# Splitting the last superblock of a graph-attention kernel into two single quads

## The chip, the cores and the metric

The kernel runs on one core of a Trainium2 chip. The metric is the device time of one execution in microseconds; a kernel's figure is the median of several runs. The core has five engines with a queue of instructions each: PE (TensorE, matrix products), DVE (VectorE), ACT (ScalarE), POOL (GpSimd) and SP (SyncE, which here issues transfers). An engine works through its queue in order and waits on semaphores for what other engines and transfers have finished.

## The reference

One layer of graph attention with a residual: 12,500 nodes of 128 values, 200,000 edges sorted by destination, four heads of 32 values.

```python
h = relu(layernorm(x))
hn = (h @ W_node.T).reshape(N, 4, 32);  e = (edge_attr @ W_edge.T).reshape(E, 4, 32)
att = sum(concat([hn[src], hn[dst], e], -1) * a, -1)      # one value per edge and head
att = where(att > 0, att, 0.2 * att)
m = maximum(segment_max(att, dst), 0.0)
ex = exp(att - m[dst])
denom = segment_sum(ex, dst) + (E - deg)[:, None] * exp(-m)   # deg: edges per destination
out = x + segment_sum((ex / denom[dst])[:, :, None] * hn[src], dst).reshape(N, 128)
```

## The kernel before

**Tiling.** The edges are cut into 392 groups of 511 (and one slot that carries the unfinished sum of the group before). Four groups are a quad (QG), so there are 98 quads, 0 to 97. A group's destinations lie in a window of 96 nodes. Quads are joined into superblocks, listed in `supers`: two of two quads, twenty of four, then 3, 3, 2, 2, 2, 2. A superblock is the unit of one softmax.

**Stages.** A first part writes a table of node rows to DRAM (h W_node and the attention terms). Then each quad goes through these steps:

- `fetch` (L472): SP loads edge attributes, destinations and the windows of x; POOL issues 16 indirect gathers, four per group, of the source nodes' rows into one of eight buffers `ga` (L137). The gathers of quad q+2 are asked for in `open_logits(q)`, and a buffer is filled again when the group that used it eight quads before is through.
- `all_logits` (L724): per group DVE compares the destinations (L500) and PE adds the destination and edge terms into `lg` (L505, L508). `flush` then calls `add_sources` (L511), which reduces `lg` (L520) and adds the gathered source term (L522) into `U`. L522 therefore waits until the quad's gathers have landed. `flush` runs at the start of the next `all_logits`, or, where there is none, at the start of the softmax.
- `softmax` (L533), once per superblock: a comparison of neighbouring destinations (`kp`, L542), transposes on PE (L547), the slope on ACT (L549), scans on DVE (L556, L566, L578, L581, L584), exponentials on ACT (L590, L593) and transposes back (L601 to L613). It yields four times between, so that other steps stand in the engines' queues among its parts.
- `sums` (L668): per group DVE scales the gathered rows (L687) and makes the one-hot marks of destinations (L691); PE sums three quarters of the group (L696). `complete_group` (L630) then adds the carry of the group before (DVE L635, ACT L639), does the last quarter (L640) and copies the result out (ACT L641). For the last two quads (FREE) POOL makes the marks (L664) early, and the carry is read from PSUM.
- `divide` (L701): denominators and quotients on DVE (L708 to L716), the addition of x (L720, on POOL for quads 95 and 96, on DVE otherwise), and one output transfer per group on SP (L722). The windows overlap, so an output is issued only when the one before it has landed. A quad's division comes in the step after its last group; the last quad is divided group by group. Each division takes a tile `res` of its own, of which there are two.

**Order.** The queues' order is written out by hand in the loop over `supers` (L795 to L811), with `together` taking one part of each step in turn. Beside the softmax of a superblock stand the sums of the quad before it and the logits of the first quad of the next superblock; beside the other sums stand the logits of the next superblock's other quads. At the end, before the change: sums of 94 beside logits of 97; sums of 95 beside the softmax of 96 and 97; sums of 96; sums of 97; outputs.

Of the kernel before, what the change touches and what calls it, by code (L numbers as in the profile page):

```python
# [8 lines left out]
F32 = mybir.dt.float32  # L9
# [9 lines left out]
D = H * HD  # L19
# [10 lines left out]
WIN = 96  # L30
QG = 4
# [15 lines left out]
def kernel(  # L47
# [51 lines left out]
    part = consts.tile([P, 1], F32, name="part")  # L99
# [20 lines left out]
    nq = len(quads)  # L120
# [27 lines left out]
    with tc.manual_schedule():  # L148
# [10 lines left out]
        with tc.tile_pool(name="prep", bufs=1) as prep, tc.tile_pool(  # L159
            name="prep_ps", bufs=1, space=bass.MemoryType.PSUM  # L160
# [127 lines left out]
        with tc.tile_pool(name="node", bufs=2) as node, tc.tile_pool(  # L288
            name="node_ps", bufs=2, space=bass.MemoryType.PSUM
        ) as node_ps, tc.tile_pool(name="index", bufs=1) as index, tc.tile_pool(  # L290
            name="index_ps", bufs=1, space=bass.MemoryType.PSUM
# [45 lines left out]
            ends = [3, 6]  # L337
# [88 lines left out]
    per = SBG // QG  # L426


    ends = [2, 2], [3, 3, 2, 2, 2, 2]
    amid = max(nq - sum(ends[0]) - sum(ends[1]), 0)  # L430
    supers = []
    for m in ends[0] + [n for _, n in blocks(amid, per)] + ends[1]:
# [5 lines left out]
    with tc.tile_pool(name="work", bufs=2) as work, \  # L438
            tc.tile_pool(name="turned", bufs=1) as turned, \
            tc.tile_pool(name="ps", bufs=1, space=bass.MemoryType.PSUM) as ps:  # L440
        XW, LG, AT, U, DR = {}, {}, {}, {}, {}
# [10 lines left out]
        def groups(s):  # L452
            q0, m = supers[s]
            g0 = quads[q0][0]
            return g0, quads[q0 + m - 1][0] + quads[q0 + m - 1][1] - g0

        def window(g):
            return nc.values_load(
                base[0:1, g:g + 1], engines=[mybir.EngineType.SP], min_val=0, max_val=N - 1,
                skip_runtime_bounds_check_because="a destination, which is a node")  # L460
# [11 lines left out]
        def fetch(q):  # L472
            if q not in EA:
                fetch_edges(q)
            fetch_windows(q)
            if q not in GA:
                gather(q, table, ROW)
# [33 lines left out]
        def add_sources(q):  # L511

            s = of_quad[q]
            g0, m = quads[q]
            s0, sm = groups(s)
            if s not in U:
                U[s] = turned.tile([P, J, SBG * H], F32, name="U", bufs=2)
            u = U[s][:, :, 0:sm * H].rearrange("p j (h g) -> p g j h", h=H)[:, g0 - s0:g0 - s0 + m]
            st = work.tile([P, QG, J, H], F32, name="st")
            nc.vector.tensor_reduce(st[:, :m], LG[q][:, :m].rearrange("p g j k h -> p g j h k"),  # L520
                                    AX.X, OP.add)
            nc.vector.tensor_tensor(u, st[:, :m], GA[q][:, :m, :, R_SRC:R_SRC + H], op=OP.add)  # L522
            for kept in (EA, DB, PW, AT, LG):
                del kept[q]
# [8 lines left out]
        def softmax(s):  # L533


            g0, m = groups(s)
            u = U.pop(s)
            R = m * H
            dr = DR.pop(s)

# [1 line left out]
            nc.vector.tensor_tensor(kp[:R, 1:GE], dr[:R, 1:NE + 1], dr[:R, 0:NE], op=OP.is_equal)  # L542
            nc.vector.memset(kp[:R, GE:GE + 1], 0.0)
            same, same_next = kp[:R, 1:GE], kp[:R, 2:GE + 1]
            t_ps = ps.tile([SBG * H, GE], F32, name="t_ps")
            for j in range(J):
                nc.tensor.transpose(t_ps[:R, j * P:(j + 1) * P], u[:, j, :R], ident)  # L547
# [15 lines left out]
            ends = turned.tile([1, H, SBG + 1], F32, name="ends")  # L563
# [66 lines left out]
        def complete_group(q, i, ga, hot, pt, acc, fc):  # L630
            g0, m = quads[q]
            g = g0 + i
            if g:
                before = state["before"]
                nc.vector.tensor_tensor(  # L635
                    ga[0:1, i, 0, 0:H * HW].rearrange("p (h w) -> p h w", w=HW),
                    before[WIN:WIN + 1, 0:H * HW].rearrange("p (h w) -> p h w", w=HW),
                    fc.unsqueeze(2).to_broadcast([1, H, HW]), op=OP.mult)
                nc.scalar.copy(ga[0:1, i, 0, R_CNT:R_CNT + 1], before[WIN:WIN + 1, R_CNT:R_CNT + 1])  # L639
            nc.tensor.matmul(acc, hot[:, i, 0, :], ga[:, i, 0, :], start=False, stop=True)  # L640
            nc.scalar.copy(pt[:, i, :], acc)  # L641
            state["before"] = acc if q >= nq - FREE else pt[:, i, :]

            if i == m - 1 or q == nq - 1:
                lo = i if q == nq - 1 else 0
                den = work.tile([WIN, QG, H], F32, name="den")
                nc.scalar.activation(den[:, lo:i + 1, :], pt[0:WIN, lo:i + 1, R_SRC:R_SRC + H],
                                     AF.Exp, scale=-1.0)
                state["division"] = q, pt, den, lo, i + 1
# [1 line left out]


        FREE = 2
        HOT = {}

        def marks(q):

            g0, m = quads[q]
            hot = work.tile([P, QG, J, WIN + 1], F32, name="hot", bufs=3)
            nc.scalar.copy(hot[:, :m, :, WIN], is_last[:, g0:g0 + m, :])  # L660
            if q >= nq - FREE:
                for i in range(m):
                    for j in range(J):
                        nc.gpsimd.tensor_scalar(hot[:, i, j, 0:WIN], lane, slot[:, g0 + i, j:j + 1],  # L664
                                                None, op0=OP.is_equal)
            return hot

        def sums(q):  # L668
# [8 lines left out]
            pt = work.tile([WIN + 1, QG, ROW], F32, name="pt", bufs=3)  # L677
            hot = HOT.pop(q) if q in HOT else marks(q)
            for i in range(m):
                nc.scalar.copy(ga[:, i, :, R_SRC:R_SRC + H], heads(xs)[:, :, :, g0 - s0 + i])  # L680
            for i in range(m):
                g = g0 + i
                if q == nq - 1 - FREE and i == 1:
                    for k in range(FREE):
                        HOT[nq - FREE + k] = marks(nq - FREE + k)
                val = ga[:, i, :, 0:H * HW].rearrange("p j (h w) -> p j h w", w=HW)
# [14 lines left out]
        def divide(q, pt, den, lo, hi):  # L701

            n = hi - lo
            xw = XW[q][:, lo:hi]
            pt = pt[0:WIN, lo:hi]
            den = den[:, lo:hi]
            others = work.tile([WIN, QG], F32, name="others")
            nc.vector.tensor_scalar(others[:, :n], pt[:, :, R_CNT], -1.0, float(E),  # L708
                                    op0=OP.mult, op1=OP.add)
            nc.vector.tensor_tensor(den, den, others[:, :n].unsqueeze(2).to_broadcast([WIN, n, H]),  # L710
                                    op=OP.mult)
            val = pt[:, :, 0:H * HW].rearrange("p g (h w) -> p g h w", w=HW)
            nc.vector.tensor_tensor(den, den, val[:, :, :, HD], op=OP.add)
            nc.vector.reciprocal(share_ps[:, :n, :], den)
            res = work.tile([WIN, QG, D], F32, name="res")
            nc.vector.tensor_tensor(  # L716
                res[:, :n, :].rearrange("p g (h d) -> p g h d", d=HD), val[:, :, :, 0:HD],
                share_ps[:, :n, :].unsqueeze(3).to_broadcast([WIN, n, H, HD]), op=OP.mult)
            add = nc.gpsimd if nq - 1 > q >= nq - 1 - FREE else nc.vector
            add.tensor_tensor(res[:, :n, :], res[:, :n, :], xw, op=OP.add)  # L720
            for i in range(n):
                nc.sync.dma_start(out[bass.ds(window(quads[q][0] + lo + i), WIN), :], res[:, i, :])  # L722
# [9 lines left out]
        def flush():  # L732

            if "logits" in state:
                add_sources(state.pop("logits"))
# [43 lines left out]
            nc.vector.tensor_copy(flag, worst[:, 2:3])  # L779
            yield  # L780

        def softmax_next(s):
            flush()
            yield from softmax(s)

        with tc.manual_schedule():
            for q in range(min(2, nq)):
                fetch(q)
            on_vector = nc.vector.tensor_copy
            together(*late(0, on_vector), normed(1))  # L790
            together(*late(1, on_vector), all_logits(0), normed(2))
            for q in range(1, supers[0][1]):
                together(all_logits(q), raw_statistics(raw_pool, 3))
            check_steps = checked()
            for s, (q0, m) in enumerate(supers):  # L795


                ahead = list(range(q0 + m, sum(supers[s + 1]))) if s + 1 < len(supers) else []
                now, ahead = ahead[:1], ahead[1:]
                together(*([sums(q0 - 1)] if s else late(2) + [raw_scaled(3)]),  # L800
                         *map(all_logits, now), softmax_next(s))
                for k in range(m - 1):
                    now, ahead = ahead[:1], ahead[1:]
                    together(sums(q0 + k), *map(all_logits, now))
                    if s > 4:
                        next(check_steps, None)
                for a in ahead:
                    together(all_logits(a))
                if not s:
                    complete()  # L810
                    together(*late(3))  # L811
            flush()
            together(sums(nq - 1))
            complete()
            complete()
            together(check_steps)
            redo = nc.values_load(flag[0:1, 0:1], min_val=0, max_val=1)
# [197 lines left out]
```

## Time and profile before

| what | value |
|---|---|
| median of 3 runs | 2048.64 us (2042.75 to 2051.03) |
| the profiled execution: own time, span | 2566.17 us, 2564.4 us |
| busy: PE, DVE, ACT, POOL | 1396.5, 1360.6, 427.9, 1514.3 us |
| granted PE clock, mean | 0.54 |
| from 300 to 2440 us: DVE busy, POOL busy | 1152.17, 1363.77 us of 2140 |
| from 2443 to 2560 us: DVE busy, POOL busy | 94.27, 19.40 us of 117 |
| last gather issued | 2440.58 us |

The profiled execution is a single one and is longer than the runs that were timed without a profile. Rows and sums from the profile are therefore compared with its own span, and only then with the median. In a row, the figure in brackets is the idle time of the engine before it and what ended it.

### The profile page before, as it was taken

The numbers are of one execution on the slowest core, as the hardware profiler recorded it, in microseconds if no ns is written. First come the engines' busy times: TensorE is split into PE (matmuls) and PEld (weight loads), VectorE is DVE, ScalarE is ACT, GpSimd is POOL, SyncE is SP. The second block draws the span as 40 slices with busy tenths as digits, with TensorE's granted clock in tenths as the row PEclk, the third lists the DMA queues.
The fourth block names the chain that finished last, engine by engine and source line by source line (L and its number), as shares of the span: only waits on it lengthen the run. The fifth ranks groups of instructions, "written<-read, shape, count | busy, mean of one in ns | idle before, by whom it ended". The sixth has DMA issues, their size and how long they took to land.

```text
span 2564.4 us, 29422 instructions
## 1 busy us (share of the span) xinstructions
PE 1396.5 (54%) x7275; PEld 1246.7 (49%) x7275; DVE 1360.6 (53%) x3314; ACT 427.9 (17%) x1777; POOL 1514.3 (59%) x1608
## 2 busy tenths in 40 slices
PE   2441665555555555556555655655555555555485
PEld 1331555554545455445454544554544554544375
DVE  2441565554554555555554654554554564455486
ACT  1441411111111111111111111111111111111122
POOL 7235256666666666666666666666666666666603
PEclk9975655555555555555555555555555555555556
DMA  4342455554554455555455545555544544544430
GB/s 152 98 130 56 113 139 124 128 125 108 131 125 111 106 140 125 129 127 124 117 127 127 124 116 126 124 122 121 122 115 120 126 120 118 123 103 112 102 93 17
DMA packets 214496, 299.12 MB, mean 117 GB/s; under 512 B 86122, under 2 KB 162154, under 8 KB 204915
## 3 DMA queue, kind: packets, MB, share of 16 engines
q1 hardware_dynamic: 162512, 184.97, 27.0%
q0 software_dynamic: 50112, 109.65, 19.7%
q10 hardware_dynamic: 1698, 2.58, 0.3%
q8 instruction: 61, 1.00, 0.2%
q14 instruction: 113, 0.92, 0.1%
HBM read 270.49 MB, written 26.52 MB: 116 GB/s over the span
## 4 chain that ended last, share of the span: by engine, by line
another core or an unknown queue 31%; PE 19%; issue 17%; DVE 15%; ACT 5%; POOL 4%; SPq 2%; DMA 1%; DVEq 0%; ACTq 0%; POOLq 0%
PE acc L696 10%; POOL ga L137 4%; PE lg L508 4%; PE acc L640 3%; DVE at L500 2%; ACT pt L641 2%; DVE res L716 1%; DVE res L720 1%; DVE hot L691 1%; DVE ga L687 1%; DVE run L556 1%; DVE ga L635 1%; PE lg L505 1%; ACT ga L639 1%
## 5 line engine op out<-in xcount | busy, mean ns | idle before, releaser
L137 POOL DMA_INDIRECT ga<-table,srci x1502 | 1433.4, 954 | 925.2 <-issue 404.5
L696 PE MATMUL acc<-ga,hot 128*97 128x137 f32 x2352 | 647.2, 446 | 346.9 <-ACT ga L680 163.7
L696 PEld LDWEIGHTS acc<-ga,hot 128*97 128x97 f32 x2352 | 515.7, 278 | 372.1 <-ACT ga L680 168.5
L635 DVE TENSOR_TENSOR ga<-pt,facs 1x132 f32<-1x132 f32 x384 | 110.7, 288 | 644.1 <-ACT pt L641 466.9
L640 PE MATMUL acc<-ga,hot 128*97 128x137 f32 x784 | 265.6, 442 | 263.1 <-ACT ga L639 127.8
L508 PE MATMUL lg<-wblk,ea 128*128 128x8 f32 x1568 | 407.8, 358 | 0.0
L641 ACT COPY pt<-acc 97x137 f32<-97x137 f32 x392 | 107.1, 273 | 1662.7 <-remote 904.7
L508 PEld LDWEIGHTS lg<-wblk,ea 128*128 128x128 f32 x1568 | 380.4, 308 | 0.0
L505 PEld LDWEIGHTS <-at 96*128 96x128 bf16 x1568 | 215.0, 165 | 295.7 <-DVE at L500 150.5
L640 PEld LDWEIGHTS acc<-ga,hot 128*97 128x97 f32 x784 | 190.7, 279 | 291.8 <-ACT ga L639 142.1
L505 PE MATMUL lg<-pw,at 96*128 96x12 bf16 x1568 | 169.5, 181 | 228.3 <-DVE at L500 123.7
L687 DVE TENSOR_TENSOR ga<-ga,ex_ps 128x528 f32<-128x528 f32 x392 | 270.1, 689 | 42.2 <-remote 35.4
L500 DVE TENSOR_TENSOR at<-const_ps,db 96x512 bf16<-96x512 f32 x392 | 266.9, 682 | 8.9 <-DMA db<-in_dst_dram 3.0
L691 DVE TENSOR_TENSOR hot<-const_ps,slot 128x384 f32<-128x384 f32 x384 | 209.1, 544 | 0.0
L520 DVE TENSOR_REDUCE st<-lg 128x64 f32<-128x192 f32 x98 | 33.7, 344 | 124.7 <-remote 79.9
L375 PE MATMUL row_ps<-wcat,hT 128*128 128x137 f32 x198 | 41.4, 361 | 80.0 <-DVE hT L367 32.8
L601 PE MATMUL ex_ps<-ident,ex 64*128 64x64 f32 (+2 forms) x112 | 18.6, 315 | 110.5 <-ACT ex L590 65.4
L375 PEld LDWEIGHTS row_ps<-wcat,hT 128*128 128x128 f32 x198 | 35.2, 253 | 86.3 <-issue 44.6
L639 ACT COPY ga<-pt 1x1 f32<-1x1 f32 x384 | 72.4, 188 | 10.7
L137 POOL DMA_INDIRECT ga<-in_x_dram,srci x64 | 60.6, 947 | 20.8 <-issue 19.2
L716 DVE TENSOR_TENSOR res<-pt,const_ps 96x512 f32<-96x512 f32 (+1 forms) x101 | 67.3, 667 | 7.1 <-DMA out_dram<-res 3.3
L601 PEld LDWEIGHTS ex_ps<-ident,ex 64*128 64x128 f32 (+2 forms) x112 | 13.8, 208 | 113.5 <-ACT ex L590 67.4
(133 smaller groups left out, 1065.2 us busy)
## 6 DMA issues: line engine op xcount, KB each, us to landing
db<-in_dst_dram SPq DMA_DIRECT2D x98, 768.0 KB
ea<-in_edge_t_dram SPq DMA_DIRECT2D x98, 512.0 KB
ga<-table,srci POOLq DMA_INDIRECT x1502
xw<-in_x_dram SPq DMA_DIRECT2D x392, 48.0 KB
out_dram<-res SPq DMA_DIRECT2D x392, 48.0 KB
pw<-side SPq DMA_DIRECT2D x392, 2.2 KB
table<-row SPq DMA_DIRECT2D x9, 616.5 KB
xt<-in_x_dram SPq DMA_DIRECT2D x9, 576.0 KB
```

What stands on the lines that cost most here:

```text
L137: nc.gpsimd.indirect_dma_start(out=ga[:, i, j, 0:width], out_offset=None, in_=rows, in_offset=bass.IndirectOffsetOnAxis(ap=srci[:, g0 + i, ...
L500: nc.vector.tensor_tensor(at[:, i, :], node_ps[0:WIN, g0 + i:g0 + i + 1].to_broadcast([WIN, GE]), db[:, i, :], op=OP.is_equal)
L505: nc.tensor.matmul(lg[:, i, j].rearrange("p k h -> p (k h)"), at[:, i, j * P:(j + 1) * P], sw, start=i + j == 0, stop=False, skip_group_ch ...
L508: nc.tensor.matmul(lg[:, i, 2 * w:2 * w + 2, 0, :], ea[:, i, w, :], wblk, start=False, stop=True, skip_group_check=True)
L635: nc.vector.tensor_tensor(ga[0:1, i, 0, 0:H * HW].rearrange("p (h w) -> p h w", w=HW), before[WIN:WIN + 1, 0:H * HW].rearrange("p (h w) -> ...
L639: nc.scalar.copy(ga[0:1, i, 0, R_CNT:R_CNT + 1], before[WIN:WIN + 1, R_CNT:R_CNT + 1])
L640: nc.tensor.matmul(acc, hot[:, i, 0, :], ga[:, i, 0, :], start=False, stop=True)
L641: nc.scalar.copy(pt[:, i, :], acc)
L687: nc.vector.tensor_tensor(val, val, heads(ex)[:, :, :, g - s0].unsqueeze(3).to_broadcast([P, J, H, HW]), op=OP.mult)
L691: nc.vector.tensor_tensor(hot[:, i, :, 0:WIN], lane_ps.unsqueeze(1).to_broadcast([P, J, WIN]), slot[:, g, :].unsqueeze(2).to_broadcast([P, ...
L696: nc.tensor.matmul(acc, hot[:, i, j, :], ga[:, i, j, :], start=j == 1, stop=False)
L716: nc.vector.tensor_tensor(res[:, :n, :].rearrange("p g (h d) -> p g h d", d=HD), val[:, :, :, 0:HD], share_ps[:, :n, :].unsqueeze(3).to_br ...
```

## The change

The last superblock of two quads (96 and 97) becomes two of one quad each. The softmax of 96 now stands beside the sums of 95 and the logits of 97, that of 97 beside the sums of 96. In `softmax` the comparison `kp` comes ahead of `flush`, which moves into it. Quad 96 is divided two groups at a time, and the parts of one quad's division write slices of one tile `res` instead of a tile each.

```diff
-    ends = [2, 2], [3, 3, 2, 2, 2, 2]
+    ends = [2, 2], [3, 3, 2, 2, 2, 1, 1]
...
             g0, m = groups(s)
-            u = U.pop(s)
             R = m * H
             dr = DR.pop(s)
...
             same, same_next = kp[:R, 1:GE], kp[:R, 2:GE + 1]
+            flush()
+            u = U.pop(s)
             t_ps = ps.tile([SBG * H, GE], F32, name="t_ps")
...
-            if i == m - 1 or q == nq - 1:
-                lo = i if q == nq - 1 else 0
+            part = 1 if q == nq - 1 else 2 if q == nq - 2 else QG
+            if (i + 1) % part == 0 or i == m - 1:
+                lo = i - i % part
...
-        HOT = {}
+        HOT, RES = {}, {}
...
-            res = work.tile([WIN, QG, D], F32, name="res")
+            if not lo:
+                RES[q] = work.tile([WIN, QG, D], F32, name="res")
+            res = RES[q][:, lo:hi]
...
-        def softmax_next(s):
-            flush()
-            yield from softmax(s)
...
-                         *map(all_logits, now), softmax_next(s))
+                         *map(all_logits, now), softmax(s))
```

## The prediction

> **What bounds the kernel now.** I read the profile's page first, then the waits of the long middle, then the last 120 us row by row. All times below, except the medians, are of the one profiled execution: 2566.2 us, of which the span is 2564.4. The median of the runs is 2048.6, 517 us less. So the first question is which of the rows also hold in a run that nobody records. The fence has two groups of the page (busy, mean ns | idle before, releaser), two lines of the waits from 300 to 2440 us (in total, times, longest), and rows in order of time (start, duration, engine, line).
>
> ```profile
> L137 POOL DMA_INDIRECT ga<-table,srci x1502 | 1433.4, 954 | 925.2 <-issue 404.5
> L641 ACT COPY pt<-acc 97x137 f32<-97x137 f32 x392 | 107.1, 273 | 1662.7 <-remote 904.7
> ...
> ACT pt L641 <- remote: 904.7, 103, 11.8
> POOL ga L137 <- remote: 226.6, 102, 3.3
> ...
> 2391.25 0.40 PE L640 MATMUL acc<-ga,hot 128*97 128x137 f32 x2
> 2399.23 0.27 ACT L641 COPY pt<-acc 97x137 f32<-97x137 f32 x1 [10.14 <-remote]
> ...
> 2386.12 0.94 POOL L137 DMA_INDIRECT ga<-table,srci  x1 [0.30 <-issue]
> 2387.36 0.94 POOL L137 DMA_INDIRECT ga<-table,srci  x1 [0.30 <-issue]
> ...
> 2440.58 0.94 POOL L137 DMA_INDIRECT ga<-table,srci  x1 [0.30 <-issue]
> ```
>
> The reader is to see three things. A gather takes 0.94 us and the next starts 1.25 us after it: 16 gathers, one quad, take 20.0 us of POOL. Once per quad (103 waits for some 94 quads) ACT starts its copy some 9 us late although the matmul it copies (2391.25) ended long before 2399.23, and what it waited for is unknown ("remote"). And those waits stop when the last gather is issued at 2440.58: among the waits after 2443 there is no "remote" row of L641.
>
> Without them the engines need 33 us for two quads: L522 of quad 93 stands at 2450.29, of 95 at 2483.30, of 97 at 2516.41, which is 16.5 us a quad. The median leaves more than that. If the last gather landed 48 us before the end (what the trace shows behind L522 of quad 97), it was at about 2048.6-1.8-48.0 = 1998.8; table gathers start at 160.96 and one wait of 49.0 us for the first free buffer stands at 289.56, so (1998.8-161-49)/1502 = 1.19 us per gather, an estimate, close under the 1.25 of the rows. So I take it that the unrecorded run is paced by POOL's gathers, and that the late copies are the recording's.
>
> Here a rule is weighed. The Trainium skill, NOTIFIC — the notification-queue block, section Overflow, says that a record queue which is full may stall the engine that produces the records. The trace agrees only in that the stalls come with the heavy traffic; no run here shows their cause. With the rule, the end is paced by gathers and my sum is -3 us; without it, engines set the end as in the trace and the sum is +4.
>
> **The end, as recorded.** These are rows in order of time; those without shapes are of the chain that ended last.
>
> ```profile
> 2483.30 0.27 DVE L522 TENSOR_TENSOR U<-st,ga 128x64 f32<-128x64 f32 x1
> ...
> 2516.41 0.27 DVE U L522
> ...
> 2532.09 0.70 DVE L687 TENSOR_TENSOR ga<-ga,ex_ps 128x528 f32<-128x528 f32 x1 [0.28 <-PE ex_ps L601]
> ...
> 2542.39 0.70 DVE L687 TENSOR_TENSOR ga<-ga,ex_ps 128x528 f32<-128x528 f32 x1
> ...
> 2547.23 1.49 DMA out_dram<-res
> 2548.73 1.50 DMA out_dram<-res
> ...
> 2553.48 0.28 DVE L716 TENSOR_TENSOR res<-pt,const_ps 96x128 f32<-96x128 f32 x1 [3.33 <-DMA out_dram<-res]
> ```
>
> L522 of 97 opens the last softmax (beside the sums of 95), L687 at 2532.09 opens the sums of 96, that at 2542.39 the sums of 97. From 2547.23 on the end is a chain of eight output DMAs, each issued when the one before it has landed (1.5 us each), and DVE waits 3.3 us in it because the third tile of quotients has to be free.
>
> **The change, part by part, on the recorded rows.** I walked the built order of the changed kernel over these rows, each instruction starting when its engine is free and its operands' rows have ended.
>
> *Logits and closing sum moved.* The logits of quad 97 and the closing of 96 (L520, L522) go from beside the sums of 94 to beside those of 95. The sums of 94 lose four L500 (pitch 0.61), 0.64 of L520 and L522, and four times 1.07 of PE's logits. The 3.1 us of DVE are not all gained: DVE waited there 0.43, 0.84 and 0.35 us for ACT and PE, and would wait more. Bounds 0.6 and 3.1; I take 2.1 (15.0 becomes 12.9).
>
> *First softmax, of quad 96 alone, beside the sums of 95 and now with the logits.* The like stage in the trace, softmax and logits together, is 2482.90 to 2501.01, 18.1 us; the one without logits 16.1 (2516.01 to 2532.09). The scans cost the same with fewer rows (1205 ns at 32 rows, 1209 at 64). I take 18.6, with the comparison ahead of the wait: +2.5. Together with the stage before, +0.4.
>
> *Second softmax, of quad 97, beside the sums of 96.* This is what the change adds. DVE's own work by the rows: four L687 2.5, four L635 1.3, comparison 0.6, L520 and L522 0.7, the multiplication part of 95's division 1.6, half a division of 96 1.3, maximum 0.7, scans 1.2, 1.3 and 1.4, the carries 1.2, column, subtraction, selection and diagonal 1.8: 15.6, and about 1.5 of waits for PE and ACT within the softmax: 17.1. Before, this stage was 10.3. So +6.8, bounds +4 (if all waits close) and +8.
>
> *Comparison ahead of the closing sum.* Where logits of another quad are due, the closing sum was already done; only the last superblock changes. It moves 0.6 us of DVE ahead of L522. Behind L522, in DVE's queue, stand the quad's L687 and L635 and all of the softmax. If L522 waits for its gather the comparison is free, else it costs up to 0.6; it is in the sums above.
>
> *Division of 96 in two, one tile of quotients per quad.* The first half's two outputs leave SP before the sums of 97, right behind the four of 95. The multiplication and addition of two groups have no row: between 0.28 (one group) and 0.68 (four) on DVE, I take 0.42; on POOL between 0.3 and 1.26, I take 0.7. The extra small instructions cost 0.9 and lie within the stage just summed. In the built order the multiplications of 97's later groups wait for DVE alone, so the 3.3 us wait is gone. From L687 of 97.0 to the last output's issue took 16.25; now six outputs remain behind the second half of 96, and I get 13.0: -3.3. [...] Two outputs taken out of the chain are worth 3.0 by the row[...].
>
> *An extra DMA:* dst rows for 97 now have a load of their own on SP, behind the outputs of 93 and ahead of those of 94. It is needed 20 us later; SP idles 6.8 us there. Nothing, or at most 0.7 us of an output's issue.
>
> Sum on the recorded execution: +0.4+6.8-3.3 = +3.9. So the changed kernel's own profile should stand near 2570 us, if the late copies are as before.
>
> **The same for the median.** With gathers in the lead the fixed points are the landings of 95 and 97, 32 gathers apart: 38.1 us at 1.19, 40.0 at 1.25. Before: L522 of 97 waits for its landing, and 48.0 us follow. After: only 33.9 us follow L522 of 97 (2534.5 to 2568.4), but DVE comes there late, 51.2 us after L522 of 95. Before 38.1+48.0 = 86.1, after 51.2+33.9 = 85.1: -1.0. At 1.25 it is -2.9; at 1.19 with engines 5% quicker unrecorded (my choice), -2.9. I take -3: 2045.5, own range 2037 to 2051.
>
> **Rivals.**
> - *Engines set the end, as in the trace* (slower than before): the second softmax costs its 6.8 us, 2048.6+4 = 2052.6, range 2049 to 2059. For it: the trace's last 120 us. Against it: 19 us a quad in the median against 16.5. It decides if DVE reaches L522 of 97 less than some 4 us before the gather lands (before it is 38.1-33.1 = 5.0).
> - *The whole gain:* if both L522 wait, 48.0-33.9 = 14 us less the outputs' chain, about -12: 2036.6. It needs landings of 95 and 97 51 us apart or engines a quarter quicker; PE's granted clock of 0.5 leaves room, DVE's rows hardly.
> - *The quotient slices still wait for DMA*, so that the split of 96 gives nothing: +3.3 on each. The built order speaks against it.
>
> **How the numbers follow.** Gather-paced 0.50, engines 0.26, whole gain 0.18, something not seen (slower) 0.06. What a measurement can tell from no change is about 0.5%, 10 us. Faster by more: 0.16 of the whole gain and 0.14 from the lower part of the first; slower by more: 0.08 of the engines' case and 0.06; 0.56 between. Range: 2035 to 2056, from the whole gain's middle to the engines' upper part.
>
> **What would show it.** In the changed profile: three stages of 12.9, 18.6 and 17.1 us ahead of L687 of 97.0; no L716 waiting for a DMA; two outputs of 96 before that L687; no late L641 copies behind the last gather. Wrong would be: a profile of the changed kernel that is not longer at its end, landings that come long before L522, or stalls that belong to the kernel and move with the new order.

## The result: 3.7 us slower, where 3 us faster was forecast

Measured side by side, the kernel before took 2046.03 us (median) and the changed kernel 2049.69 us: ratio 1.0018, 95% interval 1.0011 to 1.0026, which is +3.7 us (+2.3 to +5.3). The time lies within the predicted range, but the likeliest case had the wrong sign. Below, a ratio is turned into microseconds with 2048 us.

The changed kernel's profiled execution took 2053.09 us, with a span of 2051.3 us. So the first forecast, a profile near 2570 us if the late copies stay, is answered by its condition: the late copies are gone. Two groups of its page, and two lines of its waits from 300 to 1990 us (us in total, times, longest), answer the first fence of the prediction:

```profile
L137 POOL DMA_INDIRECT ga<-table,srci x1502 | 1443.9, 961 | 470.2 <-issue 386.4
L642 ACT COPY pt<-acc 97x137 f32<-97x137 f32 x392 | 107.4, 274 | 1267.5 <-PE acc L641 1264.3
```

```profile
ACT pt L642 <- PE acc L641: 1150.4, 344, 14.8
DVE U L522 <- DMA ga<-table,srci: 414.6, 76, 13.0
POOL ga L137 <- issue: 340.3, 1112, 1.4
```

ACT's copy (L642 here, L641 before) now waits only for the product that it copies, no longer for "remote". And DVE's closing sum, L522, waits for gathers 76 times, 414.6 us in all: POOL's gathers pace this run, as the prediction took it for the runs without a profile. No profile taken later, of either kernel, shows the late copies; what caused them in that one execution stays open.

The end of the changed kernel, in rows of DVE in order of time (start, duration, idle before in brackets). L541 is the early comparison, L689 the scaling that was L687:

```profile
1991.22 0.34 DVE L520 TENSOR_REDUCE st<-lg 128x64 f32<-128x192 f32 x1
1991.76 0.27 DVE L522 TENSOR_TENSOR U<-st,ga 128x64 f32<-128x64 f32 x1 [0.20 <-DVE st L520]
...
2010.02 0.70 DVE L689 TENSOR_TENSOR ga<-ga,ex_ps 128x528 f32<-128x528 f32 x1 [0.26 <-PE ex_ps L602]
2010.75 0.37 DVE L636 TENSOR_TENSOR ga<-pt,facs 1x132 f32<-1x132 f32 x1
2011.15 0.70 DVE L541 TENSOR_TENSOR kp<-dr 16x511 f32<-16x511 int32 x1
2011.79 0.34 DVE L520 TENSOR_REDUCE st<-lg 128x64 f32<-128x192 f32 x1
2011.80 0.06 DVE L542 MEMSET kp<- 16x1 f32 x1
2012.16 0.28 DVE L522 TENSOR_TENSOR U<-st,ga 128x64 f32<-128x64 f32 x1
```

The second L522 (2012.16) has no idle time before it. Its last gather was issued at 1996.81, and by the 2.8 us that the last one takes to land in the kernel before (1995.30 to 1998.12) the data lay there for some 12 us while DVE worked off what was queued ahead: sums of 95, logits of 97, softmax of 96. The early comparison is paid in full there (0.7 us at 2011.15), since there is no wait to hide it.

A new profile of the kernel before, taken for this comparison (2047.9 us span, no late copies), gives the other side. Both ends, cut at the same points: stretch, its length, then busy time (instructions) of PE, weight loads, DVE, ACT and POOL, granted PE clock, DMA share, GB/s. First the changed kernel, cut at L522 of 95, L522 of 97, L689 of 97.0, the issue of 96.2's output, the last output's issue, the end:

```profile
1960.77:2012.16 51.39, 33.49 (x189) 29.98 (x190) 45.61 (x108) 11.35 (x50) 42.82 (x55) 0.60 0.24 57
2012.16:2028.14 15.98, 9.70 (x45) 8.21 (x45) 12.84 (x36) 3.68 (x14) 5.52 (x9) 0.50 0.08 19
2028.14:2034.95 6.81, 5.06 (x23) 4.53 (x24) 3.92 (x11) 2.37 (x12) 0.72 (x1) 0.53 0.00 1
2034.95:2045.72 10.77, 2.66 (x18) 2.00 (x18) 6.12 (x28) 1.90 (x9) 0.00 (x0) 0.80 0.11 26
2045.72:2051.30 5.58, 0.00 (x0) 0.00 (x0) 0.00 (x0) 0.00 (x0) 0.00 (x0) 0.50 0.05 12
```

The kernel before, cut at L522 of 95, L522 of 97, L687 of 96.0 and of 97.0, the issue of 96.0's output, the last output's issue, the end:

```profile
1960.82:1998.43 37.61, 27.35 (x146) 24.84 (x146) 29.32 (x68) 7.36 (x33) 29.03 (x34) 0.50 0.31 71
1998.43:2014.14 15.71, 8.24 (x37) 6.34 (x37) 14.69 (x36) 3.00 (x11) 15.71 (x28) 0.61 0.06 14
2014.14:2024.22 10.08, 7.93 (x34) 7.35 (x35) 5.35 (x13) 2.69 (x13) 1.58 (x2) 0.50 0.02 5
2024.22:2030.48 6.26, 3.73 (x28) 3.10 (x27) 4.66 (x13) 2.44 (x13) 1.26 (x1) 0.98 0.10 25
2030.48:2041.93 11.45, 3.39 (x15) 2.45 (x13) 5.73 (x26) 1.74 (x8) 0.00 (x0) 0.53 0.13 32
2041.93:2047.90 5.97, 0.00 (x0) 0.00 (x0) 0.00 (x0) 0.00 (x0) 0.00 (x0) 0.50 0.05 14
```

From L522 of 95 to the end it is 90.5 us with the change and 87.1 us without: +3.4, close to the +3.7 of the medians. DVE's busy time in it grows from 59.75 to 68.49 us, 8.7 more, for the second softmax and the second half-division (with the split alone, below, it is 67.25 us, 7.5 more). In the first stretch DVE is busy for 45.6 of 51.4 us: no L522 in it waits for gathers any more.

### The profile page after: what moved, and what is told of

Read it like the earlier page. It is cut to its first block, busy times and chain, and to the rows that moved or that the text cites. A ratio compares the mean times of both kernels' runs of the same rounds, so it can differ in the third digit from the quotient of the medians.

```text
span 2051.3 us, 29489 instructions
## 1 busy us (share of the span) xinstructions
PE 1372.9 (67%) x7293; PEld 1246.1 (61%) x7293; DVE 1372.4 (67%) x3339; ACT 430.2 (21%) x1783; POOL 1526.6 (74%) x1609
## 4 chain that ended last, share of the span: by engine, by line
PE 28%; DVE 27%; DMA 18%; POOL 13%; issue 10%; ACT 3%; SPq 1%; DVEq 0%; ACTq 0%; POOLq 0%
PE acc L698 13%; POOL ga L137 13%; DMA ga<-table,srci 13%; PE lg L508 7%; DVE at L500 5%; PE acc L641 3%; DVE res L720 3%; DVE res L724 3%; DVE ga L689 2%; DVE hot L693 2%; DMA out_dram<-res 2%; DMA db<-in_dst_dram 2%; DVE ga L636 1%; DVE run L557 1%; PE lg L505 1%
## 5 line engine op out<-in xcount | busy, mean ns | idle before, releaser
L698 PEld LDWEIGHTS acc<-ga,hot 128*97 128x97 f32 x2352 | 517.1, 278 | 80.2 <-DVE hot L693 36.6
L642 ACT COPY pt<-acc 97x137 f32<-97x137 f32 x392 | 107.4, 274 | 1267.5 <-PE acc L641 1264.3
L522 DVE TENSOR_TENSOR U<-st,ga 128x64 f32<-128x64 f32 x98 | 26.2, 267 | 420.7 <-DMA ga<-table,srci 414.6
L689 DVE TENSOR_TENSOR ga<-ga,ex_ps 128x528 f32<-128x528 f32 x392 | 270.3, 690 | 8.8 <-PE ex_ps L602 8.3
L641 PE MATMUL acc<-ga,hot 128*97 128x137 f32 x784 | 257.1, 431 | 1.1 <-ACT ga L640 1.1
L641 PEld LDWEIGHTS acc<-ga,hot 128*97 128x97 f32 x784 | 199.2, 283 | 1.5 <-ACT ga L640 1.4
L720 DVE TENSOR_TENSOR res<-pt,const_ps 96x512 f32<-96x512 f32 (+2 forms) x102 | 67.5, 662 | 9.5 <-DMA out_dram<-res 5.7
L724 DVE TENSOR_TENSOR res<-res,xw 96x512 f32<-96x512 f32 (+1 forms) x99 | 66.6, 672 | 3.4
L682 ACT COPY ga<-xs 128x16 f32<-128x16 f32 x392 | 59.5, 214 | 0.4 <-issue 0.2
L602 PE MATMUL ex_ps<-ident,ex 64*128 64x64 f32 (+3 forms) x116 | 19.2, 312 | 59.2 <-ACT ex L591 59.2
```

The costliest lines, as they stand in the source:

```text
L689: nc.vector.tensor_tensor(val, val, heads(ex)[:, :, :, g - s0].unsqueeze(3).to_broadcast([P, J, H, HW]), op=OP.mult)
L698: nc.tensor.matmul(acc, hot[:, i, j, :], ga[:, i, j, :], start=j == 1, stop=False)
L720: nc.vector.tensor_tensor(res[:, :n, :].rearrange("p g (h d) -> p g h d", d=HD), val[:, :, :, 0:HD], share_ps[:, :n, :].unsqueeze(3).to_br ...
```

## The experiments

The theories are named in the expectations. A: gathers pace the run, and what follows the last landing, or in the changed kernel DVE's queue ahead of L522, sets the end. B: engines set the end and the gathers' landing doesn't matter. C: the loss comes from the divided division and its shared tile. D and E came later and concern the outputs.

### The kernel before, once more

> The kernel before, unchanged, profiled once more. Theory A (the gathers pace the run; what follows the last landing sets the end): no late copies this time, span near 2044 to 2049 us, last gather issued near 1997, L522 of quad 97 waits for its gather, and 45 to 48 us follow. Theory B (the engines set the end, as in the first recorded execution): L522 of 97 does not wait for a gather, or by less than 1 us. Ratio to the kernel before: 1.000 on both.

Ratio 1.0003 (0.9995 to 1.0012). DVE's rows of its profile:

```profile
1993.69 0.36 DVE L520 TENSOR_REDUCE st<-lg 128x64 f32<-128x192 f32 x1 [0.35 <-PE lg L508]
1998.43 0.32 DVE L522 TENSOR_TENSOR U<-st,ga 128x64 f32<-128x64 f32 x1 [4.38 <-DMA ga<-table,srci]
1998.64 1.03 DVE L542 TENSOR_TENSOR kp<-dr 32x511 f32<-32x511 int32 x1
```

DVE is ready at 1994.05 and waits 4.38 us for the gather issued at 1995.30; 49.5 us follow L522 (expected 45 to 48). That is theory A's picture, and it puts a number on what the gathers hide in the kernel before: 4.4 us of DVE.

### The split alone, the division alone, and everything but the split

The split alone is the first line of the change and nothing else; the division alone is its part with `part`, `lo` and `RES`. "Everything but the split" is the changed kernel with the old superblocks:

```diff
-    ends = [2, 2], [3, 3, 2, 2, 2, 1, 1]
+    ends = [2, 2], [3, 3, 2, 2, 2, 2]
```

> The change's split alone: the last superblock as one and one, quad 96 divided whole, a tile of quotients for each division, the comparison behind the closing sum. Theory A and theory B: the split is what costs (a second softmax in series on DVE), and without the earlier outputs it costs more than the whole change: 2053 us, +7 (3.7 for the whole change and 3.3 for the outputs that are not early). Theory C (the loss is in the division in halves and the shared tile, or in what they do to the outputs): about 2046 or less, since the split is then worth nothing or a gain.

> The division alone: quad 96 divided two groups at a time, one tile of quotients for each quad, superblocks as in the kernel before. Theory A and theory B: two outputs leave the final chain and the wait for the third tile goes, -3.3 us, 2043. Theory C: +3.7 or more.

> The changed kernel with its split undone (last superblock of two quads again); division in halves, shared tile and the early comparison stay. Theory A: the closing sum of 97 waits for its gather, so the comparison moves into that wait: 0.6 us less than the division alone, 2042.4. Theory B: no wait there, same as the division alone, 2043. Theory C: +3.7 or more. A difference of 0.6 us between two kernels is at the edge of what five rounds tell.

| kernel | ratio (95%) | us | expected by A |
|---|---|---|---|
| split alone | 1.0020 (1.0012 to 1.0028) | +4.1 | +7 |
| division alone | 0.9996 (0.9987 to 1.0004) | -0.8 | -3.3 |
| all but the split | 1.0000 (0.9991 to 1.0008) | 0.0 | -3.9 |
| the whole change | 1.0018 (1.0011 to 1.0026) | +3.7 | |

The split is the loss: alone it costs as much as the whole change, and without it nothing is lost. Theory C falls. But a size is off in both directions by the same thing: the division in halves and its early outputs were to bring 3.3 us and bring about half a microsecond (4.1 to 3.7 with the split, 0.8 without, neither outside its interval). Where those 3.3 us went is the question of the later runs. For the division without the split the rows give a part of the answer: in these two profiles the twelve outputs from 95.0 on leave back to back, in 18.6 us (2019.22 to 2037.83) and 17.6 us (2023.86 to 2041.42). In the new profile of the kernel before they take 19.8 us (2022.10 to 2041.93) with one step of 3.8 us, the wait for 96, where the others take 1.5 to 2.0. Only that wait, some 2.2 us, could be won. Whether the early comparison brings 0.6 us, these intervals can't tell.

### The last gathers late, and early

Late: 15 comparisons of 128x96 on POOL ahead of the gathers of quad 97, in each kernel.

```diff
             if q not in GA:
+                if q == nq - 1:
+                    pause = turned.tile([P, WIN], F32, name="pause")
+                    for _ in range(15):
+                        nc.gpsimd.tensor_scalar(pause, lane, slot[:, 0, 0:1], None, op0=OP.is_equal)
                 gather(q, table, ROW)
```

> The kernel before with 15 small comparisons on POOL (about 0.51 us each, 7.7 us in all, result unused) ahead of the gathers of quad 97, so that the last gathers land 7.7 us later. Theory A: L522 of 97 waits for them, so the end moves with them: +7.7, 2053.7. Theory B: DVE has work meanwhile, the end moves by less than 3 us.

> The changed kernel with the same 15 comparisons ahead of the gathers of quad 97. Theory A: in the changed kernel DVE comes to L522 of 97 some 13 us after the landing, so the delay is hidden: 2049.7 to 2051, and the order turns round: 3 to 4 us faster than the kernel before with the same delay. Theory B: no change either, 2049.7, but then still 3 to 4 us slower than the kernel before with the delay.

The kernel before with the delay: 1.0045 (1.0031 to 1.0059), +9.2 us. The changed kernel with it: 1.0020 (1.0009 to 1.0030), +4.1 us, no more than without. The comparisons take POOL 9.5 us, so with the last gathers some 9 us later the change *gains* about 5 us (9.2 - 4.1; from the two intervals, 1.5 to 8.7). DVE's rows, kernel before with the delay (L526 is L522 here):

```profile
1993.18 0.36 DVE L524 TENSOR_REDUCE st<-lg 128x64 f32<-128x192 f32 x1 [0.35 <-PE lg L512]
2007.37 0.30 DVE L526 TENSOR_TENSOR U<-st,ga 128x64 f32<-128x64 f32 x1 [13.84 <-DMA ga<-table,srci]
```

and the changed kernel with it:

```profile
2011.02 0.34 DVE L524 TENSOR_REDUCE st<-lg 128x64 f32<-128x192 f32 x1
2011.04 0.06 DVE L546 MEMSET kp<- 16x1 f32 x1
2011.40 0.28 DVE L526 TENSOR_TENSOR U<-st,ga 128x64 f32<-128x64 f32 x1
```

The wait grows from 4.38 to 13.84 us in the one; in the other there is still none. This is what theory B can't give: under it the delay would have moved the kernel before by less than 3 us.

Early: half of quad 96's gathers left out (8 of 16, so the result is not that of the layer), so that those of 97 start 10 us sooner.

```diff
-            for j in range(n):
+            for j in range(2 if q == nq - 2 and width == ROW else n):
```

> The kernel before without half of the gathers of quad 96 (two of four blocks of each group are left out and computed on what the buffer held before), so that those of quad 97 start 10 us earlier. Theory A: the end comes earlier until DVE is the limit, 5 us by the recorded rows: 2041. Theory B: less than 1 us.

> The changed kernel with the same half of the gathers of quad 96 left out. Theory A: nothing waits for the gathers of 97 here, so no gain, 2049.7, and the distance to the kernel before with the same cut grows from 3.7 to about 8.7 us. Theory B: no gain, distance still 3.7.

The kernel before: 0.9984 (0.9977 to 0.9990), -3.3 us. The changed kernel: 1.0009 (1.0002 to 1.0016), +1.8 us, where theory A had 3.7; this interval and that of the whole change overlap. The kernel before gains, as theory A says; it can win only the 4.4 us that DVE waited, not the 5 expected. The distance between the two kernels is 5.1 us (0.9984 to 1.0009; about 3 to 7), between the 3.7 and the 8.7 of the theories; that it grew isn't outside the intervals. The sign of the change thus hangs on one quantity, how late the last gather lands against DVE's queue: about -5 when it comes 9 us later, +3.7 as it is, +5 when it comes 10 us sooner.

### What holds the outputs back

The final outputs go one behind the other on SP. These rows of SP hold the last ones, eight in the kernel before and six behind the second half of 96 in the changed one (start, time from the first issue to the end of the last, number). First the new profile of the kernel before:

```profile
2030.48 11.77 SPq L722 DMA_DIRECT2D out_dram<-res  x8
```

and the changed kernel:

```profile
2034.95 11.10 SPq L726 DMA_DIRECT2D out_dram<-res  x6
```

Two outputs fewer save 0.67 us, not 3. An issue itself lasts 0.32 us, so eight outputs stand (11.77 - 0.32)/7 = 1.64 us apart, and the six of the changed kernel (11.10 - 0.32)/5 = 2.16. DVE was not the cause: the quotients of the last group were ready soon after 2041.65, and the last output left at 2045.72. The DMA queues of the changed kernel from 2034 to 2047 us (packets, MB, share of 16 engines) show what else moved:

```profile
q1 hardware_dynamic: 672, 0.30, 9.3%
q8 instruction: 1, 0.02, 0.8%
q14 instruction: 2, 0.02, 0.5%
```

Beside the outputs' 672 packets there are three instruction fetches, one of 16 KB and two of 8 KB. They stand where the engines come to the end of the main path, where a branch skips a general path that these inputs don't need. From the outputs of 97.0 and 97.1 to the next issue it took 2.61 and 3.36 us. Of the 112 packets of each, seven, a sixteenth, left late: at 2039.63 and at 2042.90, just as the fetches of 2039.02 to 2039.63 and of 2041.32 to 2042.91 ended. The trace does not name the DMA engine of a packet, but a sixteenth is the share of one of the 16. So theory D: the fetches hold the outputs up. The test leaves that block out, in both kernels:

```diff
-            redo = nc.values_load(flag[0:1, 0:1], min_val=0, max_val=1)
-
-    with tc.If(redo > 0):
-        tile_any_order(tc, x, src, dst, edge_t, table, side, wblk, ident, part, out, by_tile, E)
```

> The kernel before without its last block, the general path that runs only if the table's check fails (it is left out with the load and the branch that skip it; these inputs never take it). Theory D (the engines fetch instructions when they reach that branch, and these fetches hold up single packets of the last outputs): little to win here, where the outputs lost 0.4 us, so -0.4. Without theory D: no change, or the same change as for the changed kernel.

> The changed kernel without that last block. Theory D: the two outputs of 2.61 and 3.36 us come back to 1.64, so -2.7 us, and the distance to the kernel before without the block falls from 3.7 to about 1.4. Without theory D: no change, or the same change as for the kernel before, and the distance stays near 3.7.

The kernel before without it: 0.9984 (0.9977 to 0.9990), -3.3 us. The changed one: 0.9994 (0.9985 to 1.0002), -1.2 us, which is 4.9 less than the changed kernel with it. The three stretches from L689 of 97.0 on in the changed kernel without the block (columns as above):

```profile
2024.84:2031.65 6.81, 4.97 (x23) 4.53 (x24) 3.92 (x11) 2.37 (x12) 0.72 (x1) 0.60 0.00 1
2031.65:2040.45 8.80, 3.92 (x18) 2.98 (x18) 6.12 (x28) 1.90 (x9) 0.00 (x0) 0.62 0.12 29
2040.45:2042.90 2.45, 0.00 (x0) 0.00 (x0) 0.00 (x0) 0.00 (x0) 0.00 (x0) 0.50 0.09 23
```

Two effects are mixed in the runs, and the rows part them. What follows the last output's issue falls from 5.58 to 2.45 us (in the kernel before from 5.97 to 2.51): that is about 3.3 us in both, and was not expected. And in the changed kernel the six outputs take 8.80 instead of 10.77 us, while the eight of the kernel before stay (11.11 instead of 11.45). Among its fetches the 16 KB one is gone; the step beside the 8 KB one at 2035.70 still takes 2.35 us:

```profile
q1 hardware_dynamic: 672, 0.30, 9.9%
q14 instruction: 2, 0.02, 0.5%
```

Their distance goes from 3.7 to 2.0 us (0.9984 to 0.9994), where theory D said 1.4 and its absence 3.7; the intervals leave room for both, so it is the packets above and the rows, 2.0 us of outputs against 0.3, that speak for D. The size is not fixed: with the block in place the same five steps took 10.34 us in the profile with late gathers and 9.11 in that with fewer, where the 16 KB fetch fell beside the output of 97.2 and the step there took 1.91. What remains of the loss without the block, some 2 us (about 0 to 4 by the intervals), stands in these two profiles ahead of the outputs: from L522 of 95 to L689 or L687 of 97.0 it is 66.6 us with the change against 62.8, and from there to the last output's issue 15.6 against 17.3.

### Filling the wait instead

DVE waits 4.4 us ahead of the last closing sum in the kernel before. With the split undone, one or two groups more of the sums of 95 are put there.

```diff
-                together(*([sums(q0 - 1)] if s else late(2) + [raw_scaled(3)]),
-                         *map(all_logits, now), softmax(s))
+                opening = [sums(q0 - 1)] if s else late(2) + [raw_scaled(3)]
+                if s == len(supers) - 1:
+                    for _ in range(2):
+                        next(opening[0])
+                together(*opening,
+                         *map(all_logits, now), softmax(s))
```

> The changed kernel with its split undone, and one group more of the sums of 95 put ahead of the last closing sum (of 97), where DVE waits 4.1 to 4.4 us for the gather in the kernel before. Theory A: the group's DVE work (0.69 + 0.55 + 0.29 by its rows) moves into the wait: about 1.5 us less than with the split only undone, 2045.6 where that was 2047.15. Theory B: no wait to fill, no change.

> The same with two groups more. A group takes about 2.5 us there (from one L687 to the next), so DVE comes to the closing sum about 1 us after the landing. Theory A: twice 1.5 less that 1, so 2 us less than with the split only undone, 2045.1; not better than that, since the wait is used up. Theory B: no change.

Both: 0.9985 (0.9977 to 0.9994 and 0.9993), -3.1 us against the kernel before, where all but the split gave 0.0; theory A said 1.5 and 2, which the intervals do not exclude (the gain over all but the split is 0.6 to 5.6). In the profile with two groups L522 of 97 comes without a wait, 6.3 us after the last gather's issue at 1994.76:

```profile
1999.97 0.81 DVE L541 TENSOR_TENSOR kp<-dr 32x511 f32<-32x511 int32 x1
2000.71 0.34 DVE L520 TENSOR_REDUCE st<-lg 128x64 f32<-128x192 f32 x1
2000.73 0.06 DVE L542 MEMSET kp<- 32x1 f32 x1
2001.09 0.27 DVE L522 TENSOR_TENSOR U<-st,ga 128x64 f32<-128x64 f32 x1
```

So the wait is filled without a second softmax, and this beats both kernels. In it twelve outputs leave back to back from 2019.76 on, which gave theory E: where the superblock is whole, the chain begins with the outputs of 95, and two of 96 taken out of its end bring nothing there. It was tried by dividing 95 within the softmax, with its addition moved to DVE (one more line) or left on POOL; against the run with two groups ahead:

```diff
+        def closed(q):
+            yield from sums(q)
+            for _ in range(2):
+                complete()
+                yield
...
-                opening = [sums(q0 - 1)] if s else late(2) + [raw_scaled(3)]
+                opening = [(closed if s == len(supers) - 1 else sums)(q0 - 1)] if s else late(2) + [raw_scaled(3)]
```

> The kernel with the split undone and two groups of the sums of 95 ahead of the last closing sum, and now the division of 95 within the last softmax, two steps earlier, with its addition of x on DVE, since POOL is busy with marks until about 2014. Theory E (with two groups ahead, the twelve outputs from 95.0 on go out back to back, so the end hangs on when 95 is divided): the outputs of 95 start near 2010 instead of 2019.8, the last ones then wait for the engines alone: 1.6 us less than with two groups ahead alone, so -4.7 against the kernel before, less up to 0.7 for DVE's addition. Without theory E (engines set the end): no gain, or a loss of 0.7.

> The same with the addition of 95 left on POOL behind its marks. Theory E: the outputs of 95 start near 2015 to 2016, 4 us earlier than before the edit, still enough for the last outputs to wait for the engines: -4.7 against the kernel before. Without theory E: no gain, -3.1.

With the addition on DVE 0.9985 (0.9978 to 0.9992), -3.1 us: no gain, though the outputs of 95 left at 2009.63, 10 us earlier. The last eight outputs of that run, those of 96 and 97, took 4 us longer than the eight of the kernel before:

```profile
2024.65 15.74 SPq L732 DMA_DIRECT2D out_dram<-res  x8
```

With the addition on POOL 0.9977 (0.9966 to 0.9988), -4.7 us, the fastest of all, but not outside the interval of the others. Theory E is neither shown nor excluded: among the steps of these eight one of 3.01 us waits for the second half of 96, and two of 2.44 and 3.54 us stand beside a fetch of 8 KB (2030.45) and one of 16 KB (2036.08). What the earlier start gave was lost again there. With the addition on POOL the outputs of 95 left at 2018.64, not near 2015 as expected.

## Why the prediction was wrong

**Right.** The gathers pace the run, and L522 of 97 waits for them before (4.38 us) and not after. The engines' sums ahead of it were good: the three stages forecast as 12.9, 18.6 and 17.1 us took 12.7 (1978.54 to 1991.22), 18.8 (to 2010.02) and 18.1 (to 2028.14). No quotient waits for a transfer in quad 97, and two outputs of 96 leave before L689 of 97.0. The early comparison, free "if L522 waits for its gather, else it costs up to 0.6", cost 0.7.

**The sum again, with measured terms:**

| term | forecast, us | measured, us |
|---|---|---|
| before: L522 of 95 to L522 of 97 | 38.1 | 37.6 |
| before: L522 of 97 to L687 of 97.0 | 26.0 | 25.8 |
| before: L687 of 97.0 to the last output's issue | 16.25 | 17.7 |
| before: last output's issue to the end | 5.8 | 6.0 |
| changed: L522 of 95 to L522 of 97 | 51.2 | 51.4 |
| changed: L522 of 97 to L689 of 97.0 | 15.1 (33.9 - 13.0 - 5.8) | 16.0 |
| changed: L689 of 97.0 to the last output's issue | 13.0 | 17.6 |
| changed: last output's issue to the end | 5.8 | 5.6 |
| changed less before | -1.0 | +3.4 |

**The step that failed** is the one that read "from L687 of 97.0 to the last output's issue took 16.25; now six outputs remain behind the second half of 96, and I get 13.0: -3.3". That stretch took 17.7 us in the new profile of the kernel before and 17.6 us in that of the changed one: 0.1 us less, not 3.3. In the three other pairs of profiles (gathers late, gathers fewer, no general path) it went from 17.6 to 17.1, from 17.6 to 15.9 and from 17.3 to 15.6. The term of 13.0, at 17.6, is larger than the whole difference between forecast and result. Three things were mis-sized in it:

- *The row it starts from.* The rows of the recorded execution hold four L687 for the sums of 97, the last four of the program:

```profile
2541.03 0.70 DVE L687 TENSOR_TENSOR ga<-ga,ex_ps 128x528 f32<-128x528 f32 x1
...
2542.39 0.70 DVE L687 TENSOR_TENSOR ga<-ga,ex_ps 128x528 f32<-128x528 f32 x1
...
2545.78 0.69 DVE L687 TENSOR_TENSOR ga<-ga,ex_ps 128x528 f32<-128x528 f32 x1
...
2548.28 0.69 DVE L687 TENSOR_TENSOR ga<-ga,ex_ps 128x528 f32<-128x528 f32 x1
```

The row at 2542.39, which the prediction takes for 97.0, is therefore that of 97.1; 97.0 stands at 2541.03. Counted from there the stretch was 17.6 us and not 16.25, and the stage before it 8.9 and not 10.3. The sum for the changed kernel, which adds a stage that ends at 97.0 and a stretch that begins at 97.1, leaves out what lies between: 1.4 us in the recorded rows.

- *The lead to the first of the six outputs* grew from 6.26 to 6.81 us, although half a division is shorter (0.26 us on DVE, 0.54 on POOL). The chain of waits of the changed kernel shows the products of 97.0 and 96.3 there at half the clock:

```profile
2030.01 1.66 PE acc L698 x6
2031.66 0.47 PE acc L641 x2
```

against the same in the new profile of the kernel before:

```profile
2025.63 0.92 PE acc L696 x6
2026.54 0.25 PE acc L640 x2
```

That is 0.96 us. It comes with the edit: in the first 4 us behind L687 or L689 of 97.0 the granted clock is 0.50 in all five profiles with the split, and 0.97 to 1.00 in ten of the eleven without it (0.68 in the other). In the new profile of the kernel before PE was busy for 2.96 of the 3.4 us ahead of the rise of the clock (2021.00 to 2024.40); in that of the changed kernel the softmax of 97 leaves it 0.31 us of work in the 3.4 us ahead of this stretch (2024.40 to 2027.80). Whether this gap is what keeps the clock down was not tried. The rest is that the products start 1.9 us behind the scaling and not 1.4.

- *The outputs.* Two fewer of them save some 0.7 us and not 3.3 (two steps of 1.64). The five steps that remain took 10.77 us instead of 8.2. The steps beside the fetches, 2.61 and 3.36 us, hold all of this difference; without the 16 KB fetch the five took 8.80. This cost was not in the forecast at all.

**The second error was a choice, on a wrong count.** The sum with the recorded rows was -1.0; the forecast of -3 came from setting the engines 5% quicker without a profile, or the gathers at 1.25 us. The stretch of 51.2 us took 51.4 in an execution without late copies, so the engines were not quicker. The gathers did run at 1.25 us: the estimate of 1.19 took over a start at 160.96 and a wait of 49.0 us from the recorded execution, and in the new profile the first starts at 96.38 and no two are more than 1.72 us apart. But the landings of 95 and 97 are 30 gathers apart, not 32. The last of the 392 groups holds 199 edges (200,000 - 391 x 511), so it needs two gathers of 128 rows where the others need four; the 1502 gathers of the page and the 64 from x are 97 x 16 + 14. The last gather of quad 95 was issued at 1957.45 and that of 97 at 1995.30, 37.8 us later, and the two L522 stood 37.6 us apart. That 38.1 came so near was luck, too many gathers at too short a pitch. With 30 gathers at 1.25 us the prediction's own sum is 37.5 + 48.0 = 85.5 against 85.1, -0.4 and not -2.9.

**The rivals.** That the engines set the end gave the right size, +4. Of the changed kernel it is true, since nothing there waits for the last gathers; of the kernel before the delayed gathers refute it. Its threshold, DVE less than some 4 us ahead of the landing, was too low: the wait was 4.38 us and the change still lost. Between +3.7 at a wait of 4.4 us and about -5 at 13.8 us the sign turns near 8 us, if the line between them is straight. The whole gain of 12 us would have needed landings 51 us apart; they were 37.6. The rule of the Trainium skill on the full record queue (NOTIFIC — the notification-queue block, section Overflow), where stalling the engine is one of three behaviours, bears on the late copies only: no run here made or removed a full queue, and none shows whether it was the cause.

## What to carry to other kernels

Splitting a last unit of work can pay if the engine that does the extra work idles ahead of the last arrival for longer than the extra costs. Here the split added 7.5 us of DVE work: with 4.4 us of idle time it lost 3.7 us, with 13.8 us it gained about 5. Moving existing work into the 4.4 us gained about 3 us. Measure that wait in a profile without late copies first, and try the sign by delaying the arrival. Two transfers taken out of a chain at the end are not worth two of its steps unless the first of the rest can leave as early as before and nothing else, such as an engine's code at the last branch, delays them. And count rows from an end of the program before giving them a name: one row read as that of its neighbour, and a last group taken to be as full as the others, were worth 1.4 and 2.5 us here, about the size of the effect that was forecast.

## What was not expected of the hardware

- One profiled execution was 517 us longer than the runs without a profile, with a copy on ACT released 9 us late once per quad; all later profiles were within 0.3% of their medians. The cause is open.
- A general path that is never taken costs time: leaving it out with its branch took 3.3 us off the kernel before, nearly all of it behind the last output (5.97 to 2.51 us), and a fetch of 16 KB from the stretch ahead.
- Two outputs beside such fetches took 2.61 and 3.36 us instead of 1.64: seven of 112 packets left only as the fetch ended.
- The granted clock behind L687 or L689 of 97.0 was 0.50 in every profile with the second softmax ahead of it, and 0.97 to 1.00 in all but one without.
